# Integer feed-forward stage: float32r parts behind a check on the chip, in a four-layer kernel

## The chip, the cores and the metric

The kernel runs on one core of a Trainium2 chip. A core has TensorE (PE, the matmuls), VectorE (DVE), ScalarE (ACT), GpSimd (POOL) and SyncE (SP, which here only issues DMAs). The metric is device time in microseconds for one call; the kernel before takes 4647.83 us (median of three runs, 4647.5 to 4649.15).

## The reference

The input x has 4 sequences of 2048 tokens with 256 channels. Four layers follow each other, each as x = x + layernorm(layer(layernorm(x))):

```python
# 1  attention, 16 heads of 16, softmax over 2048 tokens
# 2  token-shift feed-forward: r * (relu(k)^2 @ WvT)
# 3  linear attention with its own layernorms, then gelu feed-forward (256 -> 1024 -> 256)
# 4  integer feed-forward: the weights are int32 from -127 to 127, SCALE = 1/127
gate = einsum('bsd,hd->bsh', x, w_gate * SCALE)    # HIDDEN = 768
up   = einsum('bsd,hd->bsh', x, w_up * SCALE)
out  = einsum('bsh,dh->bsd', silu(gate) * up, w_down * SCALE)
```

All of it is float32. Layer 4 is the one that changes.

## The kernel before

The kernel has two halves. The first is layer 1, attention: 16 groups (4 sequences by 4 groups of heads), each of 64 steps. A step ("tick") computes scores for the row maxima (`s`, read by DVE), scores for the softmax (`w`, read by ACT's Exp) and the weighted values (`acc`). Its score matmuls are float32r products of high and low parts (64 rows each). The second pass runs 20 ticks behind the first and the values two ticks more, so the last 22 ticks have no row maxima left. Functions can be hung on a tick with `at`. The result goes to DRAM in 16 blocks of 512 tokens, called `mids`.

The second half runs layers 2, 3 and 4 over these 16 blocks. `stage_f` is layer 2, `stage_a` and `stage_b` are the two parts of layer 3, `stage_i` is layer 4. Each is a generator whose parts have names, and a list (`FULL`, and `RAMP` for the first six periods) says in which order one period runs the parts of four different blocks: f of block p, a of block p-2, b of block p-6, i of block p-7. A period of `FULL` goes, in short: i's transposes, b's messages, gate0, a's transposes, gate1, gate2, f's k0, gate3, k1, r, b's transposes, gate4, the first gelu products, gate5, f's v, the other gelu products, b's downs, then a's keys and values with i's downs between them. PE, ACT and DVE keep exactly this program order (`InOrder`); POOL and SP are ordered by the scheduler.

A block's x is loaded once (`load`) and stays in SBUF for nine periods (pool `blocks`). `stage_i` transposes the normalized block to hT (128 channels x 512 tokens, two tiles), computes for each of six f a `gate` and an `up` product in PSUM, multiplies Silu(gate) by up into gT, and then computes four `down` products. All matmul results of the second half come from four PSUM tiles (`ps_m`, named `m` in the profile), used in turn: a product has to wait until the tile's last reader is done. Helper tiles of 512 columns come from three buffers with the tag `tmp`. `convert` loads the integer weights and multiplies them by 1/127 on DVE.

Most instructions are recorded by the helper on line 46, so the profile's lines are told apart by the names of their tiles.

Of the kernel before, what the change touches and what calls it, by code (L numbers as in the profile page):

```python
# [48 lines left out]
@with_exitstack  # L49
def sandwich_kernel(ctx: ExitStack, tc: tile.TileContext, a: dict, out: bass.AP):  # L50
# [7 lines left out]
    HID = a["wgT"].shape[1]  # L58
    NF = FF // P
    NHID = HID // P  # L60

# [12 lines left out]
    make_identity(nc, ident)  # L74
    neghalf = const.tile([P, NIT], FP, tag="neghalf", name="neghalf")
# [21 lines left out]
    b1 = vec("b1", NF)  # L97
# [44 lines left out]
    with ExitStack() as s:  # L142
# [256 lines left out]

        later, now, pending, rows, done = {}, [0], {}, [], []  # L400

# [61 lines left out]
        while later:  # L463
            now[0] = min(later)
            for fn in later.pop(now[0]):
                fn()

# [6 lines left out]
    pe, act, dve = (InOrder(tc, e) for e in (nc.tensor, nc.scalar, nc.vector))  # L474
    wpool = ctx.enter_context(tc.tile_pool(name="wpool", bufs=1))
    wq = {
        n: wpool.tile([P, rows // P, cols], FP, tag=n, name=n)
        for n, rows, cols in (("wgT", C, HID), ("wuT", C, HID), ("wdT", HID, C))
    }
    NB = B * NBLK  # L480
    LAG_A, LAG_B, LAG_I = 2, 2 + NBLK, 3 + NBLK
    blocks = ctx.enter_context(tc.tile_pool(name="blocks", bufs=LAG_I + 2))
    quer = ctx.enter_context(tc.tile_pool(name="quer", bufs=LAG_B - LAG_A + 1))
    small = ctx.enter_context(tc.tile_pool(name="small", bufs=LAG_B - LAG_A + 2))
    one = ctx.enter_context(tc.tile_pool(name="one", bufs=1))
    two = ctx.enter_context(tc.tile_pool(name="two", bufs=2))
    three = ctx.enter_context(tc.tile_pool(name="three", bufs=3))
    ps_t = ctx.enter_context(tc.tile_pool(name="ps_t", bufs=2, space=PSUM))
    ps_m = ctx.enter_context(tc.tile_pool(name="ps_m", bufs=4, space=PSUM))
    ps_kv = ctx.enter_context(tc.tile_pool(name="ps_kv", bufs=1, space=PSUM))  # L490

    def convert(name):
        wi = one.tile(list(wq[name].shape), I32, tag="gT", name="wi")
        nc.sync.dma_start(out=wi, in_=a[name].rearrange("(c p) d -> p c d", p=P))
        dve.tensor_scalar(wq[name], wi, DEQUANT, None, ALU.mult)

    kvms, vs = [], []
    for r in range(2):
        kvm = one.tile([P, CC, P + 4], FP, tag=f"kvm{r}", name=f"kvm{r}")
        nc.gpsimd.memset(kvm, 0.0)  # L500
        kvms.append(kvm)

        v = one.tile([P, CC, P + 4], FP, tag=f"v{r}", name=f"v{r}")
        nc.gpsimd.memset(v, 1.0 / T)
        vs.append(v)

    def mm_tile():
        return ps_m.tile([P, IB], FP, tag="m", name="m")

    def linear(dst, lhs, rhs, n):  # L510
        for c in range(n):
            pe.matmul(dst, lhsT=lhs(c), rhs=rhs(c), start=(c == 0), stop=(c == n - 1))

    def sums(src, tag, pool=two):
        return ln_stats(pool, [src[:, i, :] for i in range(4)], tag, dve)

    def apply(dst, src, stats):
        for i in range(4):
            ln_apply(dst[:, i, :], src[:, i, :], *stats, i, dve)

    def norm(dst, src, stats):
        mv, rs = stats
        nb = two.tile([P, 4], FP, tag="nb", name="nb")
        nc.gpsimd.tensor_tensor(nb, mv[:, :, 0], rs, ALU.mult)
        nc.gpsimd.tensor_scalar(nb, nb, -1.0, None, ALU.mult)
        for i in range(4):
            act.activation(
                dst[:, i, :],
                src[:, i, :],
                AF.Identity,  # L530
                bias=nb[:, i : i + 1],
                scale=rs[:, i : i + 1],
            )

    def to_channels(src, evac):
        for c in range(CC):
            t = ps_t.tile([P, 4, P], FP, tag="t", name="t")
            for i in range(4):
                pe.transpose(t[:, i, :], src[:, i, c * P : (c + 1) * P], ident)
            evac(c, t.rearrange("p i k -> p (i k)"))  # L540

    def block_tile(tag):
        return (three if tag == "h" else two).tile([P, 4, C], FP, tag=tag, name=tag)

    def residual(x, o):
        for i in range(4):
            nc.gpsimd.tensor_tensor(x[:, i, :], x[:, i, :], o[:, i, :], ALU.add)

    def elu1(dst, src, n):
        e = three.tile([P, IB], FP, tag="tmp", name="elu")  # L550
        dve.tensor_scalar(e[:, :n], src, 0.0, None, ALU.min)
        act.activation(e[:, :n], e[:, :n], AF.Exp)
        dve.scalar_tensor_tensor(dst, src, 0.0, e[:, :n], ALU.max, ALU.add)

    xs, before, queries, kvacc, tails = {}, {}, {}, {}, {}

    def load(j):
        xs[j] = blocks.tile([P, 4, C], FP, tag="x", name="x")
        nc.sync.dma_start(out=xs[j], in_=mids[j // NBLK][j % NBLK])


    def stage_f(j):
        x = xs[j]
        st = sums(x, "lnf")
        yield "sums"
        h = block_tile("h")
        norm(h, x, st)
        yield "norm"
        hT = one.tile([P, CC, IB + 1], FP, tag="hT", name="hT")
        if j % NBLK == 0:  # L570
            dve.memset(hT[:, :, 0:1], 0.0)
        else:
            dve.tensor_copy(hT[:, :, 0:1], tails[j - 1])
        to_channels(h, lambda c, t: act.copy(hT[:, c, 1 : IB + 1], t))
        tails[j] = two.tile([P, CC, 1], FP, tag="tail", name="tail")
        dve.tensor_copy(tails[j], hT[:, :, IB : IB + 1])
        yield "turn"
        mixed = []
        for mu, om, nm in ((mu_k, om_k, "xk"), (mu_r, om_r, "xr")):
            m = one.tile([P, CC, IB], FP, tag=nm, name=nm)  # L580
            for c in range(CC):
                w = three.tile([P, IB], FP, tag="tmp", name="shift")
                act.activation(w, hT[:, c, 0:IB], AF.Copy, scale=om[:, c : c + 1])
                dve.scalar_tensor_tensor(
                    m[:, c, :], hT[:, c, 1 : IB + 1], mu[:, c : c + 1], w, ALU.mult, ALU.add
                )
            mixed.append(m)
        xk, xr = mixed
        yield "mix"
        ka = one.tile([P, CC, IB], FP, tag="ka", name="ka")  # L590
        for d in range(CC):
            kp = mm_tile()
            linear(kp, lambda c: WkT[:, c, d * P : (d + 1) * P], lambda c: xk[:, c, :], CC)
            act.activation(ka[:, d, :], kp, AF.Relu)
            nc.gpsimd.tensor_tensor(ka[:, d, :], ka[:, d, :], ka[:, d, :], ALU.mult)
            yield f"k{d}"
        r = one.tile([P, 4, C], FP, tag="r", name="r")
        for i in range(4):
            rp = mm_tile()
            linear(  # L600
                rp[:, :C], lambda c: xr[:, c, i * P : (i + 1) * P], lambda c: WrT[:, c, :], CC
            )
            act.activation(r[:, i, :], rp[:, :C], AF.Sigmoid)
        yield "r"
        o = block_tile("o")
        for i in range(4):
            vp = mm_tile()
            linear(
                vp[:, :C], lambda c: ka[:, c, i * P : (i + 1) * P], lambda c: WvT[:, c, :], CC
            )  # L610
            dve.tensor_tensor(o[:, i, :], vp[:, :C], r[:, i, :], ALU.mult)
        yield "v"
        st = sums(o, "lno")
        yield "osums"
        apply(o, o, st)
        residual(x, o)
        yield "x"

    def affine(dst, g, be):
        return lambda c, t: act.activation(  # L620
            dst[:, c, :], t, AF.Identity, bias=be[:, c : c + 1], scale=g[:, c : c + 1]
        )


    def stage_a(j):
        x, k = xs[j], j % NBLK
        before[j] = st = sums(x, "lna", small)
        yield "sums"
        h = block_tile("h")
        norm(h, x, st)  # L630
        st = sums(h, "lnz")
        yield "norm"
        norm(h, h, st)
        yield "norm2"
        zT = three.tile([P, CC, IB], FP, tag="zT", name="zT")
        to_channels(h, affine(zT, g1, be1))
        yield "turn"
        queries[j] = QT = quer.tile([P, CC, IB], FP, tag="QT", name="QT")
        for d in range(CC):
# [19 lines left out]
        for i in range(4):  # L659
# [11 lines left out]
            if last:  # L671
                gather(*last)
# [127 lines left out]
    def step(p, stage, part):  # L800
        make, lag = MAKE[stage]
        j = p - lag
        if not 0 <= j < NB:
            return
# [76 lines left out]
```

## Time and profile before

| | us |
|---|---|
| median of three runs | 4647.83 |
| profiled execution, its own time | 4648.2 |
| its span | 4646.4 |
| attention's last matmul ends | 3069 |
| PE busy | 4378.5 (94%) |
| DVE busy | 3390.1 (73%) |
| ACT busy | 2814.3 (61%) |
| POOL busy | 968.8 (21%) |

A row of the profile's groups gives the line, the engine and operation, output and inputs by name, the shape, how many there were, their busy time together and the mean of one in ns, and at the end the idle time of the engine just before them with what ended it. A row in order of time begins with its start and its length in us; an idle time before it stands in brackets.[...]

### The profile page before, as it was taken

The page shows a single profiled execution, that of the slowest core. Times are in us where ns is not written, and L with a number is a line of the kernel's source. Part 1 is how long each engine was busy: PE and PEld are TensorE (multiplying, and loading weights), DVE is VectorE, ACT ScalarE, POOL GpSimd, SP SyncE. Part 2 cuts the span into 40 slices and gives each one's busy share as a digit, 9 for nine tenths or more (in the row PEclk, how much of TensorE's full clock was granted, in tenths as well). Part 3 has the DMA queues.
Part 4 walks back from the last instruction along what each step waited for, and adds up shares of the span by engine and source line. Part 5 has one row for each costly group of instructions (what it writes and reads, how often), then busy time and mean ns, then how long its engine had stood idle before and what let it go on. Part 6 is the DMA issues. An engine that isn't in the chain of part 4 may idle for free.

```text
span 4646.4 us, 69157 instructions
## 1 busy us (share of the span) xinstructions
PE 4378.5 (94%) x26368; PEld 2242.8 (48%) x26368; DVE 3390.1 (73%) x6838; ACT 2814.3 (61%) x3430; POOL 968.8 (21%) x1445
## 2 busy tenths in 40 slices
PE   4999999999999999999999999967899999999998
PEld 1444444444444444444444444423556666665665
DVE  4888898998899988989989889925554554543423
ACT  0777777777777777777777777744445445444232
POOL 3110111301101211001220010032333333332332
PEclk9999999999999999999999999988999999999999
DMA  3101101111001010010110110020000000000000
GB/s 105 37 11 27 31 9 40 35 35 37 15 24 32 24 56 24 15 37 16 32 42 12 30 28 10 6 75 1 1 1 19 10 10 19 10 5 10 5 10 14
DMA packets 78621, 111.34 MB, mean 24 GB/s; under 512 B 20816, under 2 KB 40656, under 8 KB 78288
## 3 DMA queue, kind: packets, MB, share of 16 engines
q1 hardware_dynamic: 71984, 103.09, 7.9%
q8 instruction: 208, 3.41, 0.3%
q10 hardware_dynamic: 6304, 3.81, 0.3%
q14 instruction: 125, 1.02, 0.1%
HBM read 22.95 MB, written 16.78 MB: 9 GB/s over the span
## 4 chain that ended last, share of the span: by engine, by line
PE 76%; DVE 14%; ACT 3%; issue 3%; POOL 2%; SPq 1%; DMA 0%; ACTq 0%; POOLq 0%; DVEq 0%
PE m L46 24%; PE acc L46 19%; PE s L46 18%; PE w L46 12%; DVE mx L46 10%; PE t L46 3%; ACT p L46 2%; ACT h L46 1%; SPq L259 1%; PE ot L46 1%; POOL hb L134 1%; DVE xm L46 1%; DVE o L46 1%; DVE lno_st L46 0%; PE kv L46 0%
## 5 line engine op out<-in xcount | busy, mean ns | idle before, releaser
L46 DVE TENSOR_REDUCE mx<-s 128x1 f32<-128x512 f32 x4096 | 2537.9, 682 | 304.8 <-PE s L46 304.7
L46 ACT ACTIVATE p<-w 128x1024 f32<-128x1024 f32 x2048 | 2003.0, 1022 | 805.4 <-PE s L46 609.3
L46 PE MATMUL s<-k,q 64*128 64x512 f32 x4096 | 1660.9, 450 | 57.2 <-DMA k<-lo 30.3
L46 PE MATMUL w<-mrow,pick 64*128 64x512 f32 x4096 | 1403.3, 416 | 0.0
L46 PEld LDWEIGHTS s<-k,q 64*128 64x128 f32 x4096 | 758.7, 186 | 1265.3 <-DVE mx L46 1148.0
L46 PE MATMUL w<-q,k 64*128 64x512 f32 x4096 | 1368.9, 419 | 0.0
L46 PE MATMUL acc<-p,xp 128*32 128x512 f32 x8192 | 1091.5, 605 | 0.0
L46 PEld LDWEIGHTS w<-mrow,pick 64*128 64x128 f32 x4096 | 748.9, 185 | 53.9
L46 PEld LDWEIGHTS w<-q,k 64*128 64x128 f32 x4096 | 669.6, 184 | 63.4 <-ACT p L46 21.2
L224 POOL TENSOR_SCALAR xd<-x,lnx_nm,lnx_rs 128x128 f32<-128x128 f32 x256 | 110.9, 448 | 990.9 <-PE t L46 990.6
L206 POOL TENSOR_SCALAR xp<-x,lnx_nm,lnx_rs 128x64 f32<-128x64 f32 x256 | 99.2, 394 | 921.3 <-PE acc L46 920.4
L46 PEld LDWEIGHTS acc<-p,xp 128*32 128x32 f32 x8192 | 161.5, 108 | 245.5 <-issue 244.3
L46 DVE TENSOR_TENSOR gT<-gs,m 128x512 f32<-128x512 f32 x96 | 65.8, 685 | 273.8 <-PE m L46 234.4
L46 PE MATMUL m<-w2T,hf 128*128 128x256 f32 x1024 | 225.6, 379 | 0.0
L46 PE MATMUL m<-zT,w1T 128*128 128x512 f32 x512 | 225.0, 592 | 0.4 <-ACT zT L46 0.4
L46 PEld LDWEIGHTS m<-w2T,hf 128*128 128x128 f32 x1024 | 194.6, 190 | 38.4 <-issue 13.4
L46 ACT ACTIVATE hf<-m,b 128x512 f32<-128x512 f32 x128 | 87.9, 687 | 170.9 <-PE m L46 170.8
L46 PE MATMUL m<-hT,wgT 128*128 128x512 f32 x384 | 183.1, 600 | 0.4 <-DVE hT L46 0.3
L46 PE MATMUL m<-hT,wuT 128*128 128x512 f32 x384 | 180.7, 593 | 0.0
L46 PE MATMUL m<-wdT,gT 128*128 128x256 f32 x768 | 173.8, 379 | 0.0
L46 ACT ACTIVATE elu<-elu 128x256 f32<-128x256 f32 (+1 forms) x96 | 46.7, 486 | 188.3 <-DVE elu L46 188.1
L46 ACT ACT_TABLE_LOAD x102 | 130.9, 1283 | 48.1 <-DVE elu L46 28.2
(130 smaller groups left out, 3675.3 us busy)
## 6 DMA issues: line engine op xcount, KB each, us to landing
q<-hi SPq DMA_DIRECT2D x256, 64.0 KB, 2.1
k<-hi SPq DMA_DIRECT2D x256, 64.0 KB, 2.1
q<-lo SPq DMA_DIRECT2D x256, 64.0 KB, 2.1
k<-lo SPq DMA_DIRECT2D x256, 64.0 KB, 2.1
x<-in_x SPq DMA_DIRECT2D x16, 512.0 KB, 5.7
mid<-x SPq DMA_DIRECT2D x16, 512.0 KB, 2.6
x<-mid SPq DMA_DIRECT2D x16, 512.0 KB, 4.9
out<-x SPq DMA_DIRECT2D x16, 512.0 KB, 2.8
```

What stands on the lines that cost most here:

```text
L46: return lambda *args, **kw: self._tc.keep_in_program_order(method(*args, **kw))
L134: dve.tensor_scalar(dst, src, mv[:, i, 0:1], rs[:, i : i + 1], ALU.subtract, ALU.mult)
L206: nc.gpsimd.tensor_scalar(heads(n)[:, i, :, :HD], xs[b][:, i, g * GH * HD : (g + 1) * GH * HD].rearrange("p (h d) -> p h d", d=HD), nm[:, ...
L224: nc.gpsimd.tensor_scalar(xd[:, i], xh.unsqueeze(1).broadcast_to([P, 2, GH * HD]), nm[:, it : it + 1], rs[:, it : it + 1], ALU.add, ALU.mult,)
L259: nc.sync.dma_start(out=dst.bitcast(FP)[r::4, cols], in_=part.bitcast(FP)[c0 : c0 + 32, :])
```

## The change

The second half becomes a function `rest`, which is built twice, once for each side of a branch. The attention half moves into `sandwich_kernel` as it was.

At tick 1025 a new function `narrow_weights` loads the three integer matrices, converts them, takes the largest magnitude over everything with DVE and one PE transpose, and writes a flag: 1 if it is at most 2047.5[...]. After attention every engine loads the flag and branches. On the false side `rest` computes as before. On the true side:

- `convert` leaves the weights as integers, in float32r tiles.
- hT is rounded to float32r by a copy on ACT, and DVE subtracts it from the float32 transpose, which gives the rest, hL. Gate and up are the sums of integer products with hT and with hL.
- The factor 1/127 moves into Silu's scale and into the product with `up`.
- The product is written over gs; ACT copies it to gT (float32r), and POOL computes the rest gL. The downs sum products with gT and gL, scaled by 1/127 in the copy from PSUM.

On both sides, x no longer stays in SBUF: f stores its block back to `mids`, and b loads it again. Two pools of three tiles (`early`, `late`) replace the pool of nine, and r takes the tile of xk.

```diff
-        r = one.tile([P, 4, C], FP, tag="r", name="r")
+        r = one.tile([P, 4, C], FP, tag="xk", name="r")
...
         residual(x, o)
+        nc.sync.dma_start(out=mids[j // NBLK][j % NBLK], in_=x)
         yield "x"
...
-        hT = three.tile([P, CC, IB], FP, tag="zT", name="hT")
-        to_channels(h, lambda c, t: dve.tensor_copy(hT[:, c, :], t))
+        hT = three.tile([P, CC, IB], FR if narrow else FP, tag="zT", name="hT")
+        if narrow:
+            hL = one.tile([P, CC, IB], FR, tag="hL", name="hL")
+
+        def evac(c, t):
+            if narrow:
+                act.copy(hT[:, c, :], t)
+                dve.tensor_tensor(hL[:, c, :], t, hT.bitcast(FP)[:, c, :], ALU.subtract)
+            else:
+                dve.tensor_copy(hT[:, c, :], t)
+
+        to_channels(h, evac)
+        parts = (hT, hL) if narrow else (hT,)
+        scale = DEQUANT if narrow else 1.0
...
-                linear(dst, lambda c: w[:, c, f * P : (f + 1) * P], lambda c: hT[:, c, :], CC)
+                products(
+                    dst,
+                    [
+                        (w[:, c, f * P : (f + 1) * P], part[:, c, :])
+                        for c in range(CC)
+                        for part in parts
+                    ],
+                )
             gs = three.tile([P, IB], FP, tag="tmp", name="gs")
-            act.activation(gs, gp, AF.Silu)
-            dve.tensor_tensor(gT[:, f, :], gs, up, ALU.mult)
+            act.activation(gs, gp, AF.Silu, scale=scale)
+            if narrow:
+                dve.scalar_tensor_tensor(gs, up, scale, gs, ALU.mult, ALU.mult)
+                act.copy(gT[:, f, :], gs)
+                nc.gpsimd.tensor_tensor(gL[:, f, :], gs, gT.bitcast(FP)[:, f, :], ALU.subtract)
+            else:
+                dve.tensor_tensor(gT[:, f, :], gs, up, ALU.mult)
...
-            act.copy(o[:, i, :], yp[:, :C])
+                [
+                    (part[:, f, i * P : (i + 1) * P], wq["wdT"][:, f, :])
+                    for f in range(NHID)
+                    for part in parts
+                ],
+            )
+            act.activation(o[:, i, :], yp[:, :C], AF.Copy, scale=scale)
...
                 if p + 1 < NB:
-                    load(p + 1)
+                    load(p + 1, early)
+                if 0 <= p + 1 - LAG_B < NB:
+                    load(p + 1 - LAG_B, late)
...
+    def products(dst, pairs):
+        for i, (lhs, rhs) in enumerate(pairs):
+            pe.matmul(dst, lhsT=lhs, rhs=rhs, start=(i == 0), stop=(i == len(pairs) - 1))
...
+        def narrow_weights():
+
+            top = att.tile([P, 3], FP, tag="top", name="top")
+            space = att2.tile([P, NIT, C], FP, tag="x", name="space")
+            for i, name in enumerate(("wgT", "wuT", "wdT")):
...
+                wi = wi.bitcast(I32)
+                nc.sync.dma_start(out=wi, in_=a[name].rearrange("(c p) d -> p c d", p=P))
+                dve.tensor_scalar(wf, wi, DEQUANT, None, ALU.mult)
+                dve.tensor_reduce(top[:, i : i + 1], wf, AX.XY, ALU.max, apply_absolute_value=True)
+            one = att.tile([P, 1], FP, tag="top1", name="top1")
+            dve.tensor_reduce(one, top, AX.X, ALU.max)
+            t = ps_1.tile([P, IB], FP, tag="s", name="t")
+            pe.transpose(t[:1, :P], one, ident)
+            most = att.tile([1, 1], FP, tag="most", name="most")
+            dve.tensor_reduce(most, t[:1, :P], AX.X, ALU.max)
+            dve.tensor_scalar(flag, most, 2047.5 * DEQUANT, None, ALU.is_le)
...
+        later[NGB * STEPS + 1] = [narrow_weights]
...
+        narrow = nc.values_load(flag, min_val=0, max_val=1)
...
+    with tc.If(narrow == 1) as branch:
+        rest(tc, a, out_rows, mids, env, True)
+    with branch.Else():
+        rest(tc, a, out_rows, mids, env, False)
```

## The prediction

> **What bounds the kernel now.** I read the slices of the page first, then the busy times of stretches (columns: PE, its weight loads, DVE, ACT, POOL, granted clock, DMA).
>
> ```profile
> PE   4999999999999999999999999967899999999998
> PEclk9999999999999999999999999988999999999999
> 3500.00:3800.00 300.00, 295.26 (x1082) 189.72 (x1081) 148.35 (x456) 144.16 (x235) 105.82 (x146) 1.00 0.03 11
> ```
>
> Attention fills the first 3069 us and keeps its instructions. In the second half PE is busy 98%, DVE 49%, ACT 48%: PE's order is the path. A full period (f, a, b and i parts) is 88.3 us, the distance of two `out` stores (3930.77 to 4019.44, likewise before). Next, what the integer stage's matmuls take in the groups and in order of time:
>
> ```profile
> L46 PE MATMUL m<-hT,wgT 128*128 128x512 f32 x384 | 183.1, 600 | 0.4 <-DVE hT L46 0.3
> ...
> 3921.50 1.88 PE L46 MATMUL m<-hT,wgT 128*128 128x512 f32 x4
> 3923.22 1.88 PE L46 MATMUL m<-hT,wuT 128*128 128x512 f32 x4
> 3924.93 1.88 PE L46 MATMUL m<-xk,WkT 128*128 128x512 f32 x4
> ...
> 3890.86 2.75 PE L46 MATMUL m<-wdT,gT 128*128 128x256 f32 x12
> ```
>
> 384 records are 16 blocks x 6 f x 2 c x 2: a float32 matmul leaves two records. Start to start, four take 1.72 us, so 0.43 per record, 0.86 per matmul of 512 columns; twelve of 256 columns take 2.59. Per block: gates 12 x 1.72 = 20.6, downs 4 x 2.59 = 10.4. Then the float32r rows, in attention:
>
> ```profile
> 2001.86 0.61 PE L46 MATMUL w<-mrow,pick 64*128 64x512 f32 x2
> 2002.09 0.61 PE L46 MATMUL s<-k,q 64*128 64x512 f32 x2
> 2002.32 0.62 PE L46 MATMUL w<-q,k 64*128 64x512 f32 x2
> ```
>
> One record per matmul, and a pair on the two row halves starts every 0.23 us[...].
>
> **The matmuls.** Each float32 product becomes two float32r ones (hi and lo part): 48 of 512 columns and 48 of 256 a block. No row has float32r on 128 rows[...]. I take 0.216, nearest in kind. For 256 columns the row of `kvm` (132 columns, float32) shows a load and a matmul every 0.120, the float32 down every 0.216; I take 0.12. So gates 10.4, downs 5.8: 14.8 us less PE work a block, 237 in 16. This is the saving only if nothing else becomes late, so I walked one period through the queues.
>
> **What is added beside them.** Per block ACT gains 2 copies of hT (0.53, row `hT<-t`) and 6 of gT (0.55 to 0.6, rows `oT`, `gs`): 4.6 us on 42.7. On DVE two subtractions (0.65 to 0.69) replace two copies, and scalar_tensor_tensor replaces tensor_tensor (both 0.69). POOL gains 6 subtractions of 1.04 (row `ka`), 6.2 on 31. All have room on average. But they stand in the queues: ACT's copy of gT waits for DVE's product, and the next Silu, the k relu and the sigmoids are queued behind it; the four PSUM tiles `m` come free only when those have read them.
>
> ```profile
> 3925.97 1.37 DVE L46 TENSOR_SCALAR o<-o,lno_mv,lno_rs 128x256 f32<-128x256 f32 x4
> 3928.03 2.08 ACT L46 ACTIVATE h<-hb,nb,lnb_rs 128x256 f32<-128x256 f32 x4 [0.58 <-POOL nb L525]
> 3930.01 0.57 ACT L46 ACTIVATE gs<-m 128x512 f32<-128x512 f32 x1
> 3932.00 0.60 ACT L46 ACTIVATE ka<-m 128x512 f32<-128x512 f32 x1 [1.42 <-PE m L46]
> ```
>
> **Walk of a full period** (times after 3900; i's transposes start at 10.8 in both). hL delays DVE's `msg` chain by 0.7; gate0 starts at 14.2 (13.7 before). gate1 and gate2 end at 20.3 (24.9). k0 needs the tile that Silu 1 reads; Silu 1 is behind copy 0, two zT and four shifts, each 0.6 to 0.75, and ends at 22.3: PE waits 2.0. k1 needs the tile of product 2, which is behind DVE's statistics of b and the four `o` (27.7): waits 1.95. r's second tile needs Silu 3, behind copy 2, the relu and b's norm (31.5): waits 1.2. gate4 starts at 35.2 (36.1), and b's first up at 37.0 (39.6). v's third tile needs Silu 5 (45.4): waits 0.9. b's second up starts at 47.2, 2.7 earlier than now. So of 10.2 us in the gates 2.7 arrive. Up to b's down3 all is PE's own: kv0 starts at 74.8 (77.5).
>
> From there the downs would save 4.6, but i's next normalization hangs on b's last down by a chain that doesn't shrink (here as it ends a period of the tail):
>
> ```profile
> 4453.36 4.85 POOL L134 TENSOR_SCALAR hb<-x,lna_mv,lna_rs 128x256 f32<-128x256 f32 x4
> 4458.17 1.04 POOL L130 TENSOR_TENSOR lno_rs<-lno_ve,neghalf 128x4 f32<-128x4 f32 x1
> ...
> 4466.19 0.33 PE L46 MATMUL t<-ident,h 128*128 128x128 f32 x1 [3.84 <-ACT h L46]
> ...
> 4468.78 3.04 PE L46 MATMUL m<-kvm,QT 128*128 128x132 f32 x16
> ```
>
> Down3 ends at 4451.8 and `h` starts at 4465.5: 13.7 to 14 us. In the full period this gives h at 89.5 instead of 96.5 (3908.19 + 88.3), and the next period starts at 92.2: length 81.4, saving 6.9.
>
> **The other periods.** Nine have all four stages: 9 x 6.9 = 62. Two have a, b, i: the same queues save about 4.5 in the gates and 4 at the end: 2 x 8 = 16. Four have b and i: the gates save 4.5 (b's turn waits for b's norm on ACT), the downs nothing, since PE already waits 3.84 there for the chain above, and the longer gap costs 1 more of slow clock: 4 x 3.5 = 14. The last has i alone: a gate goes at ACT's and DVE's pace (Silu, product, copy: 1.9 against 3.44), the first down waits for POOL's last subtraction, and 32.8 becomes 18.3: 14.5. Sum 106.6.
>
> **The check.** The first wgT load is issued early, behind `mid2_3` on SP. At tick 1025, in attention's tail where the row maxima are over, DVE converts and reduces three matrices, and PE's transpose of their maxima stands in PE's order before the rest of the tail. The second load waits for the first conversion, the third for the second.
>
> ```profile
> 3084.37 0.38 SPq L494 DMA_DIRECT2D wi<-in_wgT  x1
> 3089.72 0.96 DVE L46 TENSOR_SCALAR wgT<-wi 128x1536 f32<-128x1536 int32 x1 [0.29 <-DMA wi<-in_wgT]
> ```
>
> From issue to conversion 5.35, conversion 0.96; a reduce of 1536 about 1.75, scaled from 0.68 for 512. After the finish's two DVE steps (0.75): 0.96 + 5.4 + 0.96 + 5.5 + 0.96 + 1.75 + 0.3 = 16.6 us in which PE stands, with Exp and the values queued behind it. Nothing covers it: the tail's ticks are PE's (2.2 us each). Bounds: 12 (loads in 3) to 20. DVE's sums of the finish and POOL's stores are queued behind too, but are needed only 25 us later.
>
> Restarting costs something. In the row above, after 3.84 us idle, `kvm` took 3.04 instead of 1.97.[...]
>
> **The branch.** All engines load the flag and branch. No row shows it.[...] Below: nothing, since DVE waits 15.0 and PE 23.1 there for `mid` and `x` anyway, and the true side follows directly[...]. I take 2, and 1 for the jump at the end.
>
> **Edits at nothing.** The x tiles go back to `mids` after f and are loaded again for b: 16 stores (2.6) and 16 loads (4.9) at a DMA share of 0.03. The late load waits on SP for i's out store, and f's store is queued behind it; f's store is read four periods later, the late load is needed some 60 us later by b's `hb`. Uncovered, a late load would cost 5 per period. `r` in `xk`'s tile waits for k1's matmuls, which stand before it on PE. Scale in Silu and Copy: same rows.
>
> **Sum.** 4646.4 - 106.6 + 18.3 + 3 = 4561; the profiled execution has 1.8 around its span, and the median is 0.4 below it: 4562.
>
> **Rivals.** (1) PE stays the bound: every wait of the walk is hidden. For: ACT and DVE at 48%. Against: four `m` tiles, and the chain of 14 us. 237 - 21 saved: 4431. (2) The hand-offs cost more: downs bound by weight loads of 190 ns (48 x 0.19 = 9.1), and each copy 0.3 dearer; about 3.5 a full period, 4 and 2 in the others, 10 in the last: 58 - 21: 4611. (3) Slower: a float32r matmul on all 128 rows takes as long as a float32 record, 0.43. Then two are as dear as one float32 matmul, and the check is pure loss: 4669. It decides from where the saving falls to 21, 1.3 a block: at about 0.40. Against: the pairs start every 0.23. (4) The change doesn't act: the flag is 0 and the float32 branch runs. The integers reach 127 and the bound is 2047.5, so it needs a fault: 4669.
>
> **How the numbers follow.** Walk 0.67 (own range 4515 to 4600), rival 1 0.12, rival 2 0.13, rival 3 0.06, rival 4 0.02. The range leaves out rival 1 and the two slow ones (0.20): 4470 to 4620. A measurement tells 0.2% from no change: faster 0.91, same 0.01, slower 0.08.
>
> **What would show it.** One record per `m<-hT,wgT` matmul, four in 0.87; `out` stores 81 us apart; PE idle before `xk` and `WrT` released by ACT's gs; a PE idle of 16 us before the 1x128 transpose; the idle of 3.84 at 8 or more. Wrong if the stores lie 74 apart (PE bound), 85 or more (hand-offs), or if the check's idle is hidden.

## The result, and the profile after

The changed kernel takes 4576.2 us (median of four runs, 4575.3 to 4578.15) against 4648.0 for the kernel before: a ratio of 0.985, with an interval from 0.983 to 0.986. That is 71.8 us faster; 86 were forecast. The profiled execution has a span of 4574.2 us.

The page of the kernel after (slices, and POOL's new group), then the busy times of the same stretch as before the change (columns: PE, its weight loads, DVE, ACT, POOL, granted clock, DMA share, GB/s):

```profile
PE   4999999999999999999999999984789899899887
PEclk9999999999999999999999999997999999999998
...
L382 POOL TENSOR_TENSOR gL<-gs,gT 128x512 fp32r<-128x512 f32 x96 | 124.4, 1296 | 198.3 <-ACT gT L46 198.2
```

```profile
3500.00:3800.00 300.00, 277.53 (x1181) 191.24 (x1179) 157.62 (x489) 166.13 (x284) 142.39 (x180) 1.00 0.08 27
```

PE was busy 295 of these 300 us and is now busy 278: it waits 7.5% of the time, while each of the others still has more than 40% to spare. No engine is the bound; the order of their queues is. The matmuls themselves did what was forecast. In order of time, the kernel after, a gate and a down:

```profile
3971.95 0.40 PE L46 MATMUL m<-hL,wgT 128*128 128x512 f32 x1
3972.19 0.40 PE L46 MATMUL m<-hT,wgT 128*128 128x512 f32 x1
...
3951.76 0.28 PE L46 MATMUL m<-wdT,gL 128*128 128x256 f32 x1
3951.87 0.28 PE L46 MATMUL m<-wdT,gT 128*128 128x256 f32 x1
```

There is one record per matmul. The records overlap (0.40 us long, 0.23 apart), so the pace is read from start to start. 512 columns start every 0.23 us (0.216 forecast, the author's estimate), 256 columns every 0.117 (0.12 forecast). A block's 48 and 48 take 48 x 0.233 + 48 x 0.117 = 16.8 us instead of 31.0, so PE has 14.2 us less to do, 227 in 16 blocks. Less than half of that became time, since the check takes 17.5 and the rest went into waits.

The starts of the `out` stores divide the time by period. Two of them, one full period apart, in the kernel after:

```profile
3823.86 0.39 SPq L404 DMA_DIRECT2D out<-x  x1
...
3905.70 0.39 SPq L404 DMA_DIRECT2D out<-x  x1
```

| part | forecast | measured | from |
|---|---|---|---|
| nine full periods | -62 | -59 | 88.3 to 81.9; eight between stores, the first taken at the same 6.4 |
| two periods a, b, i | -16 | -11.0 | 77.4, 76.5 to 71.6, 71.3 |
| four periods b, i | -14 | -7.2 | 69.9, 69.1, 68.7, 61.7 to 66.9, 67.6, 67.3, 60.4 |
| last store's distance | -14.5 | -8.8 | 25.6 to 16.8 |
| check | +18.3 | +17.5 | from the `ot` transposes ahead of it to attention's last, 44.8 (3023.45 to 3068.24) to 62.3 (3024.37 to 3086.68) |
| attention ahead of the check | 0 | +0.9 | 3023.45 to 3024.37; between 3022.7 and 3025.5 in all runs here |
| branch and end jump | +3 | -0.9 | the idle before the first `h`, 23.1 to 22.1; after the last store 3.9 to 4.0 |
| first periods, no i yet | 0 | -4 | what is left of the sum |

The last row is mostly scatter: from the first `h` to the first `kvm` it is 213.6 us before, 211.4 after, and 212.1 and 215.9 in two experiments that left these periods alone.

The waits of a full period, kernel after, in order of time, first ACT's queue and then PE:

```profile
3974.58 0.62 ACT L46 CAST gT<-gs 128x512 fp32r<-128x512 f32 x1 [1.13 <-DVE gs L46]
3975.11 1.44 ACT L46 ACTIVATE zT<-t,be,g 128x512 f32<-128x512 f32 x2
3976.44 1.33 ACT L46 ACTIVATE shift<-hT,om_k 128x512 f32<-128x512 f32 x2
3977.67 1.32 ACT L46 ACTIVATE shift<-hT,om_r 128x512 f32<-128x512 f32 x2
3978.89 0.58 ACT L46 ACTIVATE gs<-m 128x512 f32<-128x512 f32 x1
3979.53 1.98 PE L46 MATMUL m<-xk,WkT 128*128 128x512 f32 x4 [1.18 <-ACT gs L46]
...
3984.80 1.98 PE L46 MATMUL m<-xk,WkT 128*128 128x512 f32 x4 [1.43 <-DVE gs L46]
...
3988.39 3.00 PE L46 MATMUL m<-WrT,xr 128*128 128x256 f32 x12 [0.74 <-ACT gs L46]
```

Copy 0 of gT waits for DVE's product; behind it stand zT, the shifts and Silu 1 (3978.89). PE needs the tile that Silu 1 reads, and waits 1.18 us for it. This is the walk of the prediction, wait for wait: 2.0, 1.95, 1.2 and 0.9 were forecast, and 1.2, 1.4, 0.7 and 0.4 came.

The end of the same kind of period, one earlier, and the chain that the prediction said would not shrink:

```profile
3951.91 4.85 POOL L537 TENSOR_SCALAR hb<-x,lna_mv,lna_rs 128x256 f32<-128x256 f32 x4
3956.73 1.04 POOL L533 TENSOR_TENSOR lno_rs<-lno_ve,neghalf 128x4 f32<-128x4 f32 x1
3957.80 2.23 DVE L46 TENSOR_SCALAR o<-o,lno_mv,lno_rs 128x256 f32<-128x256 f32 x4 [1.40 <-POOL lno_rs L533]
3959.95 0.41 DVE L46 TENSOR_SCALAR elu<-m 128x256 f32<-128x256 f32 x1
...
3964.99 0.38 ACT L46 ACTIVATE v<-m 128x256 f32<-128x256 f32 x1 [0.55 <-DVE K L46]
3965.43 0.72 PE L46 MATMUL kv<-v,K 128*128 128x132 f32 x4 [1.44 <-ACT v L46]
3965.53 2.07 ACT L46 ACTIVATE h<-x,nb,lni_rs 128x256 f32<-128x256 f32 x4
```

POOL's four hb steps hold lno's power step. DVE waits 1.40 us for that, and a's elu is queued behind it on DVE, so v is late and PE waits 1.44. The chain to `h` (3965.53) runs on beside it.

### The profile page after: what moved, and what is told of

Its sections match the earlier page's. It is cut to its first block, busy times and chain, and to the rows that moved or that the text cites. A ratio compares the mean times of both kernels' runs of the same rounds, so it can differ in the third digit from the quotient of the medians.

```text
span 4574.2 us, 69494 instructions
## 1 busy us (share of the span) xinstructions
PE 4196.7 (92%) x26369; PEld 2196.9 (48%) x26369; DVE 3394.8 (74%) x6847; ACT 2874.5 (63%) x3558; POOL 1089.5 (24%) x1541
## 4 chain that ended last, share of the span: by engine, by line
PE 60%; DVE 21%; ACT 9%; POOL 5%; issue 4%; SPq 1%; DMA 1%; ACTq 0%; POOLq 0%; DVEq 0%
PE acc L46 19%; PE s L46 17%; PE w L46 13%; DVE mx L46 10%; PE m L46 8%; PE t L46 2%; ACT p L46 2%; DVE o L46 2%; ACT h L46 2%; POOL hb L537 2%; ACT L46 1%; DVE gs L46 1%; SPq L662 1%; ACT elu L46 1%; PE ot L46 1%
## 5 line engine op out<-in xcount | busy, mean ns | idle before, releaser
L46 DVE SCALAR_TENSOR_TENSOR gs<-m,gs 128x512 f32<-128x512 f32 x96 | 66.2, 690 | 226.9 <-ACT gs L46 205.6
L382 POOL TENSOR_TENSOR gL<-gs,gT 128x512 fp32r<-128x512 f32 x96 | 124.4, 1296 | 198.3 <-ACT gT L46 198.2
L46 PE MATMUL t<-ident,h 128*128 128x128 f32 x512 | 90.2, 312 | 88.5 <-ACT h L46 55.9
L46 PEld LDWEIGHTS m<-zT,w1T 128*128 128x128 f32 x512 | 97.4, 190 | 110.6 <-issue 99.3
L140 POOL TENSOR_TENSOR x<-x,o 128x256 f32<-128x256 f32 x192 | 141.8, 767 | 17.9 <-DVE o L46 17.9
```

Source lines behind the costliest of these rows:

```text
L46: return lambda *args, **kw: self._tc.keep_in_program_order(method(*args, **kw))
L382: nc.gpsimd.tensor_tensor(gL[:, f, :], gs, gT.bitcast(FP)[:, f, :], ALU.subtract)
```

## The experiments

Distances of the `out` stores and times of all kernels that ran; a range is given where the full periods differ:

| kernel | median us | ratio to before | full period | a, b, i (mean of 2) | b, i (mean of 3) |
|---|---|---|---|---|---|
| before | 4648.0 | | 88.3 | 77.0 | 69.2 |
| after | 4576.2 | 0.985 | 81.9 | 71.4 | 67.3 |
| e1 no check | 4559.5 | 0.981 | 81.9 | 71.3 | 67.4 |
| e2 late transpose | 4559.1 | 0.981 | 81.9 | 71.4 | 67.2 |
| e3 float32 branch | 4665.2 | 1.004 | 88.3 | 77.0 | 69.3 |
| e5 hb at the end | 4554.0 | 0.980 | 80.4 | 70.2 | 64.1 |
| e6 later copies | 4563.4 | 0.982 | 79.8 to 81.5 | 70.7 | 66.4 |
| e7 gates only | 4582.7 | 0.987 | 82.5 to 84.2 | 71.9 | 66.1 |
| e8 before, hb at the end | 4634.7 | 0.997 | 88.3 | 77.0 | 64.9 |
| e9 high parts only | 4564.2 | 0.982 | 82.1 to 82.6 | 69.8 | 64.4 |
| e10 fillers | 4569.4 | 0.983 | 81.9 | 71.5 | 65.1 |
| e11 six tiles | 4559.7 | 0.981 | 80.4 | 71.2 | 67.2 |
| e12 three edits | 4520.3 | 0.973 | 78.8 | 69.5 | 63.3 |
| e13 all edits | 4490.9 | 0.966 | 77.3, one 78.0 | 68.6 | 61.3 |

All edits below are to the kernel after, except e8. The theory in all of them is the prediction's: queue order, the chain at the end of a period and the check set what arrives. The rivals are that PE's work does, or that a cost was put in the wrong place.

### e1: no check and no branch

```diff
-        later[NGB * STEPS + 1] = [narrow_weights]
...
-        narrow = nc.values_load(flag, min_val=0, max_val=1)
...
-    with tc.If(narrow == 1) as branch:
-        rest(tc, a, out_rows, mids, env, True)
-    with branch.Else():
-        rest(tc, a, out_rows, mids, env, False)
+    rest(tc, a, out_rows, mids, env, True)
```

> The check and the branch are left out: the integer weights are taken as small without being looked at, and the new second half follows attention directly. Theory (the check stands on the path with its 14.75 us of PE idle and some 3.7 us of slow clock behind it, the branch costs nothing): attention's last transposes come 18.4 us earlier, the idle before the second half grows by about 1 and everything after it keeps its times: 4576 - 17.4 = 4559 us. Rival A (what follows attention is held by something else, so the idle only moves to the start of the second half): 4570 or more. Rival B (the branch has a price that the first transposes don't show, 3 to 6 us): 4552 to 4556.

Measured: 4559.5, 16.7 less than after, where 17.4 were expected. The first `h` comes at 3092.16, where it was before the change (3092.02), and the idle ahead of it is 23.2 again. So the check costs its stall and the restart behind it, and the branch nothing that can be seen.

### e2: only PE's part of the check later

```diff
+            later[NGB * STEPS + 99] = [lambda: write_flag(one)]
+
+        def write_flag(one):
             t = ps_1.tile([P, IB], FP, tag="s", name="t")
             pe.transpose(t[:1, :P], one, ident)
```

> Only PE's part of the check moves: the transpose of the maxima, the last reduction and the flag come after attention's last transposes; loads, conversions and reductions stay where they are. Theory (the idle is only PE's place in the order; DVE's chain of 15 us lies under 20 ticks of PE work if PE doesn't wait for it): PE idle of 14.75 and the slow clock are gone, one transpose and about 1 us of hand-off are added in the 22 us in which PE waits for x anyway: 4576 - 18 = 4558 us. Rival (the finish steps, sums and stores that are queued on DVE behind the check come late, hold the tiles that the second half reuses, and take back the gain): 4570 to 4576.

Measured: 4559.1, as fast as without a check. First the kernel after at the check, then e2, both in order of time:

```profile
3036.73 0.96 DVE L46 TENSOR_SCALAR space<-space 128x1536 f32<-128x1536 int32 x1 [2.93 <-DMA space<-in_wdT]
...
3039.72 0.37 PE L46 MATMUL t<-ident,top 128*1 128x128 f32 x1 [14.75 <-DVE top L46]
...
3040.03 1.94 PE L46 MATMUL acc<-p,xp 128*32 128x512 f32 x8
...
3043.90 1.94 PE L46 MATMUL acc<-p,xp 128*32 128x512 f32 x8
...
3109.39 2.80 PE L46 MATMUL t<-ident,h 128*128 128x128 f32 x8 [22.06 <-DMA x<-mid]
```

```profile
3068.82 0.66 PE L46 MATMUL ot<-ident,oT 128*128 128x128 f32 x4 [0.69 <-ACT oT L46]
3069.31 0.27 PE L46 MATMUL t<-ident,top 128*1 128x128 f32 x1
...
3091.61 0.47 PE L46 MATMUL t<-ident,h 128*128 128x128 f32 x1 [22.02 <-DMA x<-mid]
```

The same transpose waits 14.75 us in one place and not at all in the other, where the whole check lies under attention's tail and the 22 us in which PE waits for x. The loads, conversions and reductions on DVE cost nothing once PE doesn't stand in front of them. After the long idle, eight `acc` matmuls take 1.94 instead of 1.06 (at 3032.99 in the kernel before): PE runs at half pace, and the granted clock from 3039.7 to 3045.7 is 0.50. Of the 17.5 us of the table, 14.75 are the idle, 0.3 the transpose and the remaining 2.5 the restart.

### e3: the float32 side of the branch

```diff
-            dve.tensor_scalar(flag, most, 2047.5 * DEQUANT, None, ALU.is_le)
+            dve.tensor_scalar(flag, most, 2047.5 * DEQUANT, None, ALU.is_gt)
```

> The comparison of the check is turned round, so that the flag is 0 and the float32 branch runs, with the check, the branch and the extra stores and loads of x. Theory (check 18.4, branch -1, the 16 stores and 16 late loads hidden): 4648 + 17.4 = 4665 us, out stores 88.3 apart in the full periods. Rival (the late loads or r in the tile of xk cost time in every period, some 2 to 5 us in 11 periods): 4690 to 4720, stores 90 to 93 apart.[...]

Measured: 4665.2, and the full periods are 88.3 apart as in the kernel before. The check, the branch, the 16 stores and the 16 late loads of x and `r` in the tile of xk together cost 17.8 us against the kernel before that ran beside it (4647.4). The check explains it: it takes 16.5 here, measured as in the table, and attention came to it 1.5 later than in the kernel before. The prediction's edits at nothing are at nothing. This is also what the prediction gave for its fourth rival, 4669.

### e5: the hb steps last on POOL

The hb steps become the last part of a period and are pinned in POOL's order:

```diff
-        "a:kv0 next:b.pre i:down0 b:osums a:kv1 i:down1 b:x a:kv2 next:a.norm2 i:down2 next:i.sums "
-        "a:kv3 i:down3 a:kv4 next:i.norm"
+        "a:kv0 i:down0 b:osums a:kv1 i:down1 b:x a:kv2 next:a.norm2 i:down2 next:i.sums "
+        "a:kv3 i:down3 a:kv4 next:i.norm next:b.pre"
...
-            ln_apply(hb[:, i, :], x[:, i, :], mv, rs, i, nc.gpsimd)
+            ln_apply(hb[:, i, :], x[:, i, :], mv, rs, i, InOrder(tc, nc.gpsimd))
```

> b's four hb steps on POOL (4.85 us together), which stand ahead of the power step of lno, are made the last step of the period, behind i's nb. Theory (the end of a period hangs on the chain from b's last down over POOL's hb, lno, x, lni to ACT's h): h comes 4.85 us earlier. In the b and i periods the idle of 8.57 shrinks by 4 to 5, but b's messages then wait for hb by 1 to 2: 4 x 3; in the full periods PE's waits of 0.3 + 1.4 + 1.1 + 0.6 at the end go in part, 9 x 2; 2 x 1.5 and 4 in the others: 37 in all, 4539 us. Rival (PE's work and the waits at the four tiles m set the period, the chain only touches PE at the end): full periods keep 81.9, only the tail gains, 4560 to 4565. Second rival (late hb delays b's messages and its norm by as much): 4576.

Measured: 4554.0, a gain of 22; 37 were expected. The period's end in order of time, e5:

```profile
3949.96 1.04 POOL L533 TENSOR_TENSOR lno_rs<-lno_ve,neghalf 128x4 f32<-128x4 f32 x1 [3.37 <-DVE lno_ve L46]
3951.09 2.20 DVE L46 TENSOR_SCALAR o<-o,lno_mv,lno_rs 128x256 f32<-128x256 f32 x4
3953.21 0.41 DVE L46 TENSOR_SCALAR elu<-m 128x256 f32<-128x256 f32 x1
...
3958.69 0.72 PE L46 MATMUL kv<-v,K 128*128 128x132 f32 x4 [0.42 <-ACT v L46]
```

DVE no longer waits for lno's power step, and PE waits 0.42 behind v instead of 1.44. A full period gives 1.5 and not 2; the waits behind hT and zr stay. In the b and i periods 3.2 arrive, as the idle ahead of i's transposes goes from 8.57 to 5.29. So in the full period the chain cost time through DVE's queue, by 1.5, and was not itself what PE waited for; in the tail it was.

### e8: the same edit in the kernel before

> The kernel before, with only the order on POOL changed: b's hb steps become the last of the period, as in the run of the changed kernel, where that took 1.5 us from each full period and about 3.3 from the b and i periods. Theory (in the full periods of the kernel before, PE's float32 downs cover POOL's order, so it only became a cost with the change): full periods stay 88.3, the four b and i periods give 3.3 each and the two with a, b and i nothing: 4648 - 13 = 4635 us. Rival (it was a cost all along and has nothing to do with the change): 22 less as there, 4626.

Measured: 4634.7, 12.7 less than before (4635 expected). The full periods stay at 88.3 and the b and i periods fall by 4.3. POOL's order cost nothing in the full period until the downs became shorter, so that wait was made by the change. The tail's part was there all along: with this edit the float32 kernel's b and i periods (64.9) are shorter than those of the changed kernel.

### e6: the copies of gT one gate later

```diff
-                dve.scalar_tensor_tensor(gs, up, scale, gs, ALU.mult, ALU.mult)
-                act.copy(gT[:, f, :], gs)
-                nc.gpsimd.tensor_tensor(gL[:, f, :], gs, gT.bitcast(FP)[:, f, :], ALU.subtract)
+                g[f] = early_g[:, f, :] if f < 4 else gs
+                dve.scalar_tensor_tensor(g[f], up, scale, gs, ALU.mult, ALU.mult)
+                for k in {0: (), 4: (3, 4), 5: (5,)}.get(f, (f - 1,)):
+                    act.copy(gT[:, k, :], g[k])
+                    nc.gpsimd.tensor_tensor(
+                        gL[:, k, :], g[k], gT.bitcast(FP)[:, k, :], ALU.subtract
+                    )
```

> For the first four f, ACT's copy of the product to gT and POOL's gL come one gate later, behind the next Silu; the product waits in the tile that later holds hf. Nothing is left out. Theory (copy 0, copy 2 and the others stand in front of the next Silu on ACT and wait for DVE's product, which makes k0, r and v wait 1.2, 0.7 and 0.4 at the tiles m): these waits go down to about half, but the wait behind DVE's product (1.4 before k1) stays and takes part of it back: 1 us in each of 9 full periods, little in the others: 4566 us. Rival (the tiles are held by DVE's and ACT's other work, the copies only fill gaps): 4574 to 4578.

Measured: 4563.4 (4566 expected). The wait before k0 is 0.59 instead of 1.18, the one before k1 is gone, and r waits 0.6 and 1.5. So ACT's order was part of the gates' pace, and not all of it. Some full periods are 79.8 and some 81.5, and r is the difference. In order of time, e6, r in a period of either kind:

```profile
3576.91 4.49 PE L46 MATMUL m<-WrT,xr 128*128 128x256 f32 x12 [1.50 <-ACT gs L46]
...
3739.84 2.86 PE L46 MATMUL m<-WrT,xr 128*128 128x256 f32 x12 [1.51 <-ACT gs L46]
```

After the same wait of 1.5 us, the same twelve matmuls take 2.86 or 4.49 us; the granted clock from 3574 to 3582 is 0.79. The difference is the 1.6 between the two kinds of period. The waits around r are the same in both; what decides between the two paces was not shown.

### e7: gates in float32r, downs in float32

```diff
-                dve.scalar_tensor_tensor(gs, up, scale, gs, ALU.mult, ALU.mult)
-                act.copy(gT[:, f, :], gs)
-                nc.gpsimd.tensor_tensor(gL[:, f, :], gs, gT.bitcast(FP)[:, f, :], ALU.subtract)
+                dve.scalar_tensor_tensor(gT[:, f, :], up, scale, gs, ALU.mult, ALU.mult)
...
-        parts = (gT, gL) if narrow else (gT,)
+        parts = (gT,)
```

(wdT and gT are float32 tiles here.)

> The downs go back to float32: gT is float32 straight from DVE's product, ACT's copies of gT and POOL's gL are gone, wdT holds the integers in float32; gates and ups stay float32r in two parts. Theory (the downs' saved PE time arrives only where PE, not b's chain, ends the period): gates hand over a little faster without the copies (1 us in a full period), the downs are 4.6 longer there, of which the chain hides some 2: about +1.5 in 11 periods, 0 in the four b and i periods, whose idle of 8.57 goes back to about 4, +3 in the last: 4576 + 20 = 4596 us. Rival A (PE is the bound, the downs are worth 4.6 in every block): 4576 + 70 = 4646. Rival B (the copies cost as much as the downs bring): 4576.

Measured: 4582.7, nearer to rival B (4576) than to the theory (4596), and far from PE as the bound (4646). The downs save PE 4.8 us a block, 77 in all, and with the copies and subtractions that they need they bring 6.5 of them (4582.7 against 4576.2). In the b and i periods they cost 1.1 each (66.1 here, 67.3 with them). Without copies on ACT the gates of a full period wait 0.6 and 1.5, together 1.7 less than the 1.2, 1.4, 0.7 and 0.4 of the kernel after, and the longer downs leave no wait behind v: what the downs bring at the end, their copies take from the gates. (The two full periods of 84.2 have r at half pace, 4.54 for twelve matmuls.)

### e9: only the high parts multiplied

```diff
-        parts = (hT, hL) if narrow else (hT,)
+        parts = (hT,)
...
-        parts = (gT, gL) if narrow else (gT,)
+        parts = (gT,)
```

> Every product with hL and gL is left out on PE, so half of the integer stage's matmuls are missing and the output is only that of the high parts; hL and gL are still computed. PE has 24 x 0.232 + 24 x 0.117 = 8.4 us less in each block, 134 in 16. Theory (the gates already go at the pace of ACT's and DVE's hand-offs, and the end of a period at that of b's chain): of 8.4 little arrives, about 1 in a full period and 0 to 1 in the others: 4560 us. Rival (PE is still the bound, the waits are side effects): 4576 - 134 = 4442; halfway, 4509, if the gates are free and the downs held.

Measured: 4564.2. Half of the integer stage's matmuls are gone, 134 us of PE work, and 12 us arrive, none of them in the full periods, which even became a little longer (82.1 to 82.6 after 81.9). This is the clearest evidence against rival 1 of the prediction, that PE stays the bound. One full period of e9 in order of time, and its stretch 3500 to 3800:

```profile
3902.06 3.78 PE L46 MATMUL m<-xk,WkT 128*128 128x512 f32 x4 [3.58 <-ACT gs L46]
```

```profile
3500.00:3800.00 300.00, 262.76 (x1006) 173.04 (x1005) 154.61 (x478) 166.01 (x279) 143.26 (x181) 0.95 0.08 28
```

PE arrives at k0 earlier and waits 3.58 for the same Silu. k0's four matmuls then take 3.78 us instead of 1.98, at half pace, so the shorter work even cost something: the granted clock of the stretch is 0.95, after 1.00. In the period shown PE waits 10.9 us, where the kernel after waits 7.2; the rest of the 8.4 us that were taken out goes into half pace. So e9 shows that little arrives, but not how much would at full clock.

### e10: matmuls in the tail's idle times

```diff
+            if NB + LAG_A <= p <= NB + LAG_B - 1 and item == "b:turn":
+                warm(4)
+            if NB + LAG_A < p <= NB + LAG_I - 1 and item == "i:turn":
+                warm(9 if p < NB + LAG_I - 1 else 5)
```

(`warm(n)` multiplies `ident` by w1T n times into a tile m that nobody reads.)

> Nothing is left out; PE gets matmuls whose results nobody reads, in the idle times of the periods without f and a: 4 of 0.86 us ahead of b's transposes (idle 4.2) and 9, in the last period 5, ahead of i's (idle 8.6 and 5.3). Theory (the tail gained less than forecast because each of these idle times is followed by some 4 us at half clock, which costs 1.3 to 2 us in every period before PE is back): 5 stretches ahead of i's transposes cost about 1.5 to 2 less each, 4 ahead of b's about 1.3 less: 4576 - 13 = 4563 us. Rival (the restart is hidden behind the waits for h and zr that come with it, the rest of the shortfall is queueing): 4574 to 4578.

Measured: 4569.4, 6.8 less; 13 were expected. (The edit fills eight idle times, four of each kind; the expectation counts five ahead of i's.) A b and i period of the kernel after, then of e10, in order of time:

```profile
4406.64 2.80 PE L46 MATMUL t<-ident,h 128*128 128x128 f32 x8 [8.57 <-ACT h L46]
4409.23 2.87 PE L46 MATMUL m<-kvm,QT 128*128 128x132 f32 x16
...
4424.09 0.33 PE L46 MATMUL t<-ident,h 128*128 128x128 f32 x1 [4.17 <-ACT h L46]
```

```profile
4404.24 0.33 PE L46 MATMUL t<-ident,h 128*128 128x128 f32 x1 [0.88 <-ACT h L46]
...
4406.32 1.97 PE L46 MATMUL m<-kvm,QT 128*128 128x132 f32 x16
```

With the idle filled, `kvm` takes 1.97 instead of 2.87, and a b and i period is 2.2 us shorter (mean of three). So the slow clock after the two idle times (granted, in the kernel after, 0.50 from 4406.64 to 4408.64 and 0.58 from 4424.1 to 4428.2) is worth this much in the tail; one of the two the kernel before pays as well, after its idle of 3.84. In the last period i alone gained nothing from it: the end moves by 6.0 where its transposes came 6.9 earlier. Its gates wait 1.59 for a product instead, and the downs wait as before.

### e11: one pool of six PSUM tiles

```diff
-    ps_t = ctx.enter_context(tc.tile_pool(name="ps_t", bufs=2, space=PSUM))
-    ps_m = ctx.enter_context(tc.tile_pool(name="ps_m", bufs=4, space=PSUM))
+    ps_m = ctx.enter_context(tc.tile_pool(name="ps_m", bufs=6, space=PSUM))
...
-            t = ps_t.tile([P, 4, P], FP, tag="t", name="t")
+            t = ps_m.tile([P, 4, P], FP, tag="m", name="t")
```

> The two PSUM tiles of the transposes and the four tiles m become one pool of six, used in turn; nothing else changes. Theory (PE waits at k0, k1, r and v for a tile that was handed out four products earlier; with six it may run one or two products further ahead): the 3.8 us of these waits in a full period go down by about 2, part of it comes back at the end of the period: 1.2 in 9 full periods, less in the others: 4563 us. Rival A (PE is only let ahead into the next wait, since ACT and DVE set the pace of the gates): 4574 to 4578. Rival B (the transposes now wait behind products in the common pool): 4580 to 4600.

Measured: 4559.7, 16.5 less (13 expected), and a full period is 80.4, which gives 13.5 in nine. (The first store comes 7.7 earlier, only 1.5 of it from a full period, and the last store's distance is 2.2 longer.) The number fits the theory, but the place doesn't. PE's waits in a full period ahead of i's gate0, kernel after:

```profile
3968.13 1.14 PE L46 MATMUL t<-ident,h 128*128 128x128 f32 x8 [1.11 <-ACT hT L46]
...
3971.64 0.47 PE L46 MATMUL m<-hT,wgT 128*128 128x512 f32 x1 [0.57 <-DVE zr L46]
```

And the waits of e11 from the same place on:

```profile
3951.47 0.77 PE L46 MATMUL t<-ident,h 128*128 128x128 f32 x5 [0.16 <-ACT h L46]
3961.38 1.98 PE L46 MATMUL m<-xk,WkT 128*128 128x512 f32 x4 [0.77 <-DVE xk L46]
3968.19 2.28 PE L46 MATMUL m<-WrT,xr 128*128 128x256 f32 x8 [0.39 <-DVE gs L46]
3971.78 1.13 PE L46 MATMUL m<-WrT,xr 128*128 128x256 f32 x4 [1.31 <-ACT gs L46]
3973.66 0.66 PE L46 MATMUL t<-ident,h 128*128 128x128 f32 x4 [0.31 <-ACT ka L46]
```

With 1.04 ahead of gate4, the gates wait 3.8 us in e11, as they do in the kernel after. What went is the 1.11 and 0.57 ahead of gate0: i's transposes no longer wait for the tiles of f's. That wait is older than the change: at the same place the kernel before waits 1.58 (3910.79); what six tiles would bring there was not tried. Of the gates rival A is true. PE is only let ahead into the next wait; they go at the pace of ACT and DVE, and the four tiles m are where that shows, not its cause.

### e12 and e13: together

e12 is e2, e5 and e6 in one kernel. e13 adds the six tiles and fillers of 3 and 5 matmuls, sized for e12's idle times.

> The late transpose of the check, the hb steps at the end of the period and the later copies of gT together. Theory (three different places: 17 alone, 22 alone, 13 alone): the later copies gave 2.0 only in those full periods in which no wait behind v took 1.45 back, and the hb edit removes just that wait, so the sum is a little more than the parts: 4576 - 56 = 4520 us. Rival (the two edits in the period compete for the same wait): 4576 - 17 - 25 = 4534.

> The three edits of the run before this, with the common pool of six PSUM tiles and with filler matmuls in the tail (3 ahead of b's transposes, whose idle was 3.5 with the three edits, and 5 ahead of i's, whose idle was 5.3). Theory (each names another wait): the waits left in a full period of the three edits are 0.6, 0.6 and 1.5 at the tiles m and 2.1 at its end; six tiles take about 1.3 of them in 9 periods, the fillers 1.2 in each of four periods and 2 at the last: 4520 - 12 - 7 = 4501 us. Rival A (with the later copies in place the tiles no longer hold PE, and the fillers collide with shorter idle times): 4516 to 4522. Rival B (transposes in the common pool wait behind products): above 4522.

Measured: 4520.3 (ratio 0.973, interval 0.971 to 0.974) and 4490.9 (0.966, 0.965 to 0.968). e12 falls where its expectation said, but the reason given there is wrong. In e6 the wait of 1.4 behind v stands in every full period, of either kind; what made some of them longer is r at half pace. In e12 no r is slow, after the same wait of 1.5, and its full period is 78.8 throughout. Part of the agreement is luck. PE's waits in a full period of e13:

```profile
3833.80 0.72 PE L46 MATMUL kv<-v,K 128*128 128x132 f32 x4 [0.42 <-ACT v L46]
3836.03 0.77 PE L46 MATMUL t<-ident,h 128*128 128x128 f32 x5 [0.16 <-ACT h L46]
3845.52 1.98 PE L46 MATMUL m<-xk,WkT 128*128 128x512 f32 x4 [0.37 <-DVE xk L46]
3853.03 1.13 PE L46 MATMUL m<-WrT,xr 128*128 128x256 f32 x4 [0.22 <-DVE early_g L46]
3855.68 1.13 PE L46 MATMUL m<-WrT,xr 128*128 128x256 f32 x4 [1.52 <-ACT gs L46]
3858.38 0.50 PE L46 MATMUL m<-hT,wgT 128*128 128x512 f32 x1 [0.70 <-ACT r L46]
```

Together 3.4, where the kernel after waits 7.2. e13 gave 10 more than expected: the full periods are 1.5 shorter than in e12, as in e11, but the first `out` store comes 9.7 earlier, in periods that the expectation left out. e13 is 85 us faster than the changed kernel, more than the change itself brought, with the same products.

## Why the prediction was right, and where it was off

The mechanism was right: PE's saving of 227 us (237 forecast) is mostly lost in waits for ACT and DVE at the gates and at the end of each period, and of the 134 us more that e9 takes away only 12 arrive. That the sum came within 14 us is luck in part: the periods of the tail fell 17 short, and some 8 us of gains that were not forecast, in the first periods and at the branch, hid half of that. Point by point:

- **Matmuls.** One record per matmul on 128 rows, 0.233 and 0.117 us. Rival 3 (0.43) is excluded by the rows. So is the first half of rival 2: the weight loads of 190 ns don't bound the downs, which start every 117 ns.
- **Full period.** 81.4 forecast, 81.9 measured. Two terms were off against each other. The gates gave more: b's second up starts 3.5 us earlier and not 2.7. The four waits are 2.3 shorter together than walked, but the work between them is 1.5 longer, so that PE reaches some of them later (on the walk's clock gate2 ends at 20.8 and not 20.3). The end gave less: 2.9 and not 4.2. The step that failed is "13.7 to 14 us" for the chain from b's last down to `h`, read in the tail, where nothing else stands in the queues. In the full period it is 3949.45 to 3965.53, 16.1: POOL starts hb 0.7 later there, behind steps of a's norm, and DVE puts a's elu steps between (1.3). "A chain that doesn't shrink" was nearly true: up to `nb` it is 16.4 us before and 15.9 after. Most of what the end gained is that `h` in the kernel before waited 2.6 more in ACT's queue. e5 adds that the chain reached PE first through DVE's queue.
- **Gates and downs.** The walk put 2.7 of 6.9 us down to the gates; e7, with the gates alone, brings 5.8 of 6.4. The walk didn't ask what the gates would give without the downs' copies, which are paid for in the gates. And "the four PSUM tiles" as what holds them fell with e11: with six the gates wait as long.
- **Tail.** Here most of the error lies: 44.5 forecast for the six periods and the last distance, 27 measured. In a b and i period the four gates ahead of b's transposes fall from 13.7 to 7.9 us, but PE then idles 4.2 for b's norm. The prediction saw this wait and still put the gates' gain at 4.5. From gate0 to b's transposes 13.7 us became 12.2, so only 1.5 of 5.8 arrive there. What was missed is that this idle brings a second restart: the eight transposes take 2.46 until gate4 instead of 1.14. The term "the longer gap costs 1 more of slow clock" knew of one restart, where e10 puts the two at 2.2 a period.
- **Last period.** 18.3 us were forecast from its first gate to its last down; it is 24.1 (4540.0 to 4564.1), 15.1 for gates and 9.0 for downs. The step "a gate goes at 1.9" holds for four of the six. The first gate takes 3.9 at the slow clock (granted 0.50 from 4540.0 to 4543.9), and in the fifth PE waits 1.30 for DVE's product. Two downs wait 0.99 and 0.96 for gL, whose subtraction is 1.30 us and not the 1.04 of `ka`. That was a row wrongly chosen: the kernel before has 64 subtractions of gL's form in attention (`lo<-xe,hi`, 128x512 to fp32r), and they take 1.29.
- **Check.** 18.3 forecast, 17.5 measured, by two errors: the loads landed in 4.3 and 4.6 us and not 5.35, so the idle is 14.75 and not 16.6; the restart cost 2.5, more than was left for it in the 18.3 (the author's estimate, from no row). The second slow `acc` group (3043.90, again 1.94) ends 6 us after PE restarts. One run doesn't give the price of a restart: the eight kernels with this check idle 14.60 to 14.76 us and then lose 1.5 (e5) to 2.6 us (e10, e11).
- **Branch.** 2 forecast (the author's estimate, from no row), nothing seen (e1, e3). PE waits 22 us for x there, so a small cost would be covered, as the lower bound said.

What stays open: whether the branch costs anything where no wait covers it, what decides whether half pace follows an idle, and how much of PE's saving would arrive at full clock throughout.

## What to carry to other kernels

When the busiest engine gets cheaper work, walk one period through the other engines' queues before multiplying the saving by the count: here 227 us of matmul time brought some 90 before the check, and five small edits to queues, buffers and idle times afterwards brought 85. A check that needs one matmul should let that matmul stand where the engine waits anyway; its place in the order cost 17 us, its work nothing. A gap on PE can charge twice, by itself and by half pace behind it, so a saving that only lengthens a gap can be less than nothing (e9's full periods: an idle of 3.58 ahead of k0, then 3.78 instead of 1.98 for k0).

## What the runs showed of the hardware that was not expected

- A float32r matmul of 256 columns starts every 0.117 us with new weights each time, although every weight load is recorded at 0.19: the recorded loads overlap one another.
- A subtraction on POOL of 128 x 512 took 1.30 us with a float32r result and two different inputs (1.29 for `lo` in attention), where a float32 product of a tile with itself took 1.04. Which of the differences it is was not tried.
- Half pace did not go by the length of the idle alone. In four full periods of e9 k0 took 3.39 to 3.78 instead of 1.98 after idles of 3.13 to 3.58. In the kernel after, eight matmuls `m<-xk,WkT` took 3.70 at 3173.68, after 3.54 of idle and at a granted clock of 1.00. After an idle of 1.5, r's twelve matmuls took 4.49 or 2.86 in e6, and 4.54 in two periods of e7.
